# Four graph layers on one core: the order of a few TensorE steps at the layer borders

## The chip, the core and the metric

The kernel runs on 1 core of one Trainium2 chip. The metric is the time of one execution on the device in microseconds (us), as a median of several executions. The engines are named as the profile names them: PE is TensorE, DVE is VectorE, ACT is ScalarE, POOL is GpSimd, SP is SyncE (here it only issues DMAs).

## The reference

A graph of N = 3327 nodes with 512 features each and a dense 0/1 adjacency matrix goes through four layers. Each normalises the rows, applies a relu, runs a graph layer and adds the result to its input:

```python
h = relu(layernorm(x))
x = x + GAT0(h, adj)      # 8 heads of 64
h = relu(layernorm(x))
x = x + GAT1(h, adj)      # 4 heads of 128, adjacency plus the identity
h = relu(layernorm(x))
x = x + GAT2(h, adj)      # 8 heads of 64
h = relu(layernorm(x))
x = x + Mean3(h, adj)

# a head of a GAT layer
Wh = h @ W ;  s1 = Wh @ a1 ;  s2 = Wh @ a2
att = softmax over j of where(adj, leaky_relu(s1[i] + s2[j], 0.2), -inf)
out = elu(att @ Wh)

# the mean layer
agg = adj @ h / max(degree, 1)
out = relu(concat(h @ W_self + b_self, agg @ W_nb + b_nb) @ W_comb + b_comb)
```

## The kernel before

**Tiles and stages.** The nodes are 26 tiles of 128 rows (NT = 26, the last has 127), the 512 features are KC = 4 blocks of 128. A GAT layer first makes, per node tile, the projected features multiplied by exp(s2) and by exp(0.2 s2) (in three bf16 pieces, or in float32), and stores these pieces to DRAM. Then it runs over chunks of four target tiles and, inside, over the heads. For each head ACT (L694) and DVE (L691) compare s1[i] + s2[j] with zero for every source tile j, and DVE combines the outcome with the adjacency mask (`and` at L698, `xor` at L700). The two 0/1 matrices `tht` and `gt` are the stationary operands of the attention products on PE, with the pieces `ab` as moving operand: L809 and L812 in layers 0 and 2, L805 and L802 in layer 1. In layer 1 three of the five groups of source tiles are used as float32: there ACT (`ts`, L663) or DVE (`tv`) casts the 0/1 matrix first, and the products are L802. The source tiles come in groups of 6, 6, 6, 4 and 4. A chunk's four targets are worked in two passes of two; only in the first head of a layer's first chunk both passes first run over the source tiles below 22 and then over the rest, which leaves time for the last node tiles' pieces to arrive.

**The next layer's tiles.** The node work of layer l+1 is woven into the attention products of layer l. `node_stages` gives for each tile t a list of steps: load the layer's output, `statistics` (DVE, then POOL in `norm`, up to L359), `relu` (ACT, L365, makes `h`), `turn` (four PE transposes L138 into a PSUM tile `tp`, and one ACT copy L142 that makes `hT`), `projected` (eight PE matmuls in two halves of four: 264 or 272 columns with the scores, then 256 without; L420), `scaled` (ACT exponentials and DVE multiplications, L462), `parts` (the pieces on DVE, ACT and POOL), `send` (stores, issued by SP at L562). `Hooks.run` takes one step of every tile in flight between two passes. In the last chunk's run the last two tiles, 24 and 25 (NT-2 and NT-1), remain when the attention products are over: `hooks.drain()` runs their steps one after the other. This stretch between the last attention product of a layer and the first of the next one is called a border here. There are three: layer 0 to 1, 1 to 2, and 2 to 3.

**What else lies at a border.** Layer 3 is linear up to its last relu, so its weights are multiplied together ahead of time. The class `Fusion` does that, W_self @ W_comb's upper half at the first border and W_nb @ W_comb's lower half at the second. Each is four blocks of 128 rows: `block(k)` transposes a block of the weights (L138, and the copy L142), runs four matmuls of 512 columns (L191), copies the result from PSUM (L195) and stores it. `biases` is four matmuls of 512 columns (L208) whose result DVE adds to the bias (L212). Blocks 0 and 1 and the bias product stand ahead of the drain, blocks 2 and 3 behind it:

```python
        fusion = close()
        if fusion:
            for k in range(2):
                fusion.block(k, gone[-1])
            fusion.biases(gone[-1])
        adds = run_left()
        hooks.drain()
        for add in adds:
            add()
        if fusion:
            for k in range(2, KC):
                fusion.block(k, gone[-1])
```

At the third border there is no fusion. There each of tiles 22 to 25 has two projections of its own onto the multiplied weights, `project_last` with i = 1 in the tile's steps and i = 0 behind the drain (L498, four matmuls of 512 columns each). Behind them the mean layer's products start (L1077), after a small transpose (L1033).

L528 (`send_s1`) is a small transpose that turns the last chunk's scores s1 into rows. It follows tile 25's projection.

**What sets the order.** All engines' instructions are put in order at build time by a scheduler with a cost model; buffers of a pool are handed on by semaphores. `after(inst, name)` adds a dependence that only the scheduler sees: `inst` is placed behind the instruction called `name`, usually the last attention product of a pass (`gone[-1]`) or the last projection matmul (`L.mm`), and nothing waits for it at run time. On each engine the instructions then run in this fixed order, and one that waits holds up all behind it.

## Time and profile before

| | |
|---|---|
| three runs | 3471.0, 3467.43, 3469.67 us; median 3469.67 |
| the profiled execution | 3468.93 us, of which the profile's span is 3466.7 us |
| mean granted TensorE clock | 0.996 of full speed |
| busy share of the span | PE 98%, PE weight loads 89%, DVE 76%, ACT 72%, POOL 18% |
| DMA | 797.69 MB, mean 230 GB/s |
| first border (0 to 1) | from about 1167 to 1198 us of the span |
| second border (1 to 2) | from about 2012 to 2046 us |
| third border (2 to 3) | from about 3130 to 3149 us |

The times in the views are microseconds from the start of the span. A row of a timeline gives the start, the time until the group of like instructions ends, engine, line, operation, output and inputs by the program's names, sizes, the number of instructions, and in square brackets the engine's idle time just before the row with what ended it. A row of the table of windows gives the stretch, its length, the busy time of PE, PE's weight loads, DVE, ACT and POOL (with the number of rows), the granted TensorE clock as PEclk, the DMA engines' busy share and their GB/s. "Granted clock" is the share of full speed that the throttle let TensorE have.

### The profile page before, as it was taken

The numbers are of one execution on the slowest core, as the hardware profiler recorded it, in microseconds if no ns is written. First come the engines' busy times: TensorE is split into PE (matmuls) and PEld (weight loads), VectorE is DVE, ScalarE is ACT, GpSimd is POOL, SyncE is SP. The second block draws the span as 40 slices with busy tenths as digits, with TensorE's granted clock in tenths as the row PEclk, the third lists the DMA queues.
The fourth block names the chain that finished last, engine by engine and source line by source line (L and its number), as shares of the span: only waits on it lengthen the run. The fifth ranks groups of instructions, "written<-read, shape, count | busy, mean of one in ns | idle before, by whom it ended". The sixth has DMA issues, their size and how long they took to land.

```text
span 3466.7 us, 77498 instructions
## 1 busy us (share of the span) xinstructions
PE 3412.4 (98%) x30735; PEld 3092.3 (89%) x30735; DVE 2641.0 (76%) x5131; ACT 2502.6 (72%) x4125; POOL 640.6 (18%) x886
## 2 busy tenths in 40 slices
PE   8899999999999999999999999999999999999999
PEld 6799999999999788888888879989898989887887
DVE  8889888988878799889888867877776768682221
ACT  6878887878888888898888767766676757582211
POOL 7611222212111202323233320000000001021000
PEclk9999999999999999999999999999999999999999
DMA  8799999999857887787877976555555555586331
GB/s 237 237 295 279 244 268 253 259 270 261 234 194 266 294 283 259 271 287 258 287 272 268 336 258 201 190 191 162 192 175 179 185 177 186 166 299 263 104 110 55
DMA packets 398629, 797.69 MB, mean 230 GB/s; under 512 B 112969, under 2 KB 221844, under 8 KB 397616
## 3 DMA queue, kind: packets, MB, share of 16 engines
q1 hardware_dynamic: 363890, 723.14, 65.3%
q0 software_dynamic: 27488, 60.32, 7.3%
q10 hardware_dynamic: 6878, 9.18, 0.8%
q8 instruction: 244, 4.00, 0.5%
q14 instruction: 129, 1.06, 0.1%
HBM read 663.59 MB, written 129.64 MB: 229 GB/s over the span
## 4 chain that ended last, share of the span: by engine, by line
PE 90%; DVE 4%; DMA 2%; ACT 2%; issue 2%; POOL 1%; SPq 0%; ACTq 0%; POOLq 0%; DVEq 0%
PE acc L809 24%; PE acc L812 24%; PE acc L802 13%; PE acc L1077 9%; PE acc L805 6%; PE mm L420 5%; PE mm L498 5%; PE acc L420 1%; ACT gt L694 1%; PE tp L138 1%; PE mm L191 1%; DMA tr<-at 1%; DMA ab<-ab 1%; DMA w<-in_L_gnn_W_dram 0%; DVE AB L462 0%
## 5 line engine op out<-in xcount | busy, mean ns | idle before, releaser
L694 ACT ACTIVATE gt<-s1b,ks 128x512 fp8e4<-128x512 f32 (+1 forms) x2448 | 1448.2, 677 | 373.4 <-PE acc L812 262.1
L809 PE MATMUL acc<-ab,tht 128*128 128x195 bf16 (+1 forms) x9112 | 1551.2, 248 | 1.4 <-DVE deg L830 1.4
L812 PE MATMUL acc<-ab,gt 128*128 128x195 bf16 (+1 forms) x9112 | 1550.7, 248 | 1.5 <-DVE gt L700 1.5
L812 PEld LDWEIGHTS <-gt 128*128 128x128 fp8e4 x10744 | 1051.1, 98 | 22.4 <-issue 15.4
L809 PEld LDWEIGHTS <-tht 128*128 128x128 fp8e4 x10744 | 1051.2, 98 | 14.2 <-issue 5.8
L698 DVE TENSOR_TENSOR tht<-gt,m 128x768 uint32<-128x768 uint32 (+3 forms) x557 | 447.9, 804 | 101.1 <-ACT gt L694 98.6
L700 DVE TENSOR_TENSOR gt<-tht,m 128x768 uint32<-128x768 uint32 (+3 forms) x557 | 449.0, 806 | 9.5
L663 ACT CAST ts<-tht 128x1536 fp32r<-128x1536 fp8e4 x208 | 301.8, 1471 | 94.5 <-PE acc L802 87.9
L691 DVE TENSOR_SCALAR gt<-s1b,ns 128x512 fp8e4<-128x512 f32 (+1 forms) x446 | 224.9, 507 | 168.3 <-PE acc L812 167.1
L802 PE MATMUL acc<-ab,ts 128*128 128x258 f32 x2496 | 332.9, 289 | 0.6 <-DMA ab<-ab 0.4
L802 PEld LDWEIGHTS acc<-ab,ts 128*128 128x128 f32 x2496 | 312.0, 189 | 8.7 <-ACT tht L694 0.8
L925 POOL TENSOR_TENSOR xt<-xt,e 128x512 f32<-128x512 f32 x72 | 121.5, 1687 | 1053.0 <-DVE e L924 1030.0
L694 ACT ACTIVATE tht<-s1b,ks 128x512 fp8e4<-128x512 f32 (+1 forms) x504 | 309.1, 680 | 0.9 <-DMA s1b<-s 0.2
L1077 PE MATMUL acc<-y,mf 128*128 128x512 f32 x1352 | 309.6, 391 | 0.0
L1077 PEld LDWEIGHTS acc<-y,mf 128*128 128x128 f32 x1352 | 253.7, 188 | 55.7 <-issue 0.5
L812 PE MATMUL acc<-abx,gt 128*128 128x195 bf16 (+1 forms) x1632 | 283.1, 248 | 1.7 <-DVE rc L847 1.7
L809 PE MATMUL acc<-abx,tht 128*128 128x195 bf16 (+1 forms) x1632 | 283.1, 248 | 0.2 <-DVE tht L698 0.2
L827 DVE TENSOR_REDUCE R<-acc 128x130 f32<-128x390 f32 x416 | 214.4, 554 | 78.8 <-PE acc L812 77.9
L1074 ACT CAST mf<-m 128x768 fp32r<-128x768 fp8e4 (+1 forms) x78 | 59.1, 762 | 243.2 <-PE acc L1077 231.4
L805 PE MATMUL acc<-ab,tht 128*128 128x387 bf16 x1248 | 223.6, 328 | 5.9 <-DMA ab<-ab 5.9
L802 PE MATMUL acc<-ab,tv 128*128 128x258 f32 x1664 | 218.4, 283 | 0.7 <-DMA ab<-ab 0.7
L802 PEld LDWEIGHTS acc<-ab,tv 128*128 128x128 f32 x1664 | 207.1, 189 | 1.7 <-issue 0.9
(168 smaller groups left out, 3712.3 us busy)
## 6 DMA issues: line engine op xcount, KB each, us to landing
ab<-ab SPq DMA_DIRECT2D x333, 600.0 KB, 5.9
ab<-ab SPq DMA_DIRECT2D x112, 774.0 KB, 6.5
ab<-ab SPq DMA_DIRECT2D x112, 516.0 KB, 5.2
ab<-ab SPq DMA_DIRECT2D x112, 400.0 KB, 3.8
abx<-ab SPq DMA_DIRECT2D x110, 400.0 KB, 6.6
ab<-ab SPq DMA_DIRECT2D x56, 582.0 KB, 6.3
s1b<-s SPq DMA_DIRECT2D x120, 256.0 KB, 5.3
m<-mask SPq DMA_DIRECT2D x69, 384.0 KB, 4.4
```

Source lines behind the costliest of these rows:

```text
L420: mm = nc.tensor.matmul(pw, hT[:, k, :], L.w[:, k, o:e], start=(k == 0), stop=(k == KC - 1))
L663: (nc.scalar.copy if KIND[g] == "s" else nc.vector.tensor_copy)(t[:, :k1 - k0, :nj], th[a][g][:, k0:k1])
L691: nc.vector.tensor_scalar(gv[:, :, jj, :], s1v, L.ns2[:, j, h:h + 1], 2.0, op0=ALU.is_gt, op1=ALU.mult, saturate=False)
L694: nc.scalar.activation(gv[:, :, jj, :], s1v, AF.Relu, bias=L.ks2[:, j, h:h + 1], scale=BIG, saturate=False)
L698: nc.vector.tensor_tensor(pu, gu, mu, ALU.bitwise_and)
L700: nc.vector.tensor_tensor(gu, pu, mu, ALU.bitwise_xor)
L802: mm = nc.tensor.matmul(acc[k][:, :2 * DA], thr[g][:, k - ks[0], jj, :], ab[a][g][:, jj, :], start=(j == 0), stop=(j == NT - 1), skip_grou ...
L805: mm = nc.tensor.matmul(acc[k][:, :3 * DA], th[a][g][:, k, jj, :], ab[a][g][:, jj, :3 * DA], start=(j == 0), stop=(j == NT - 1), skip_grou ...
L809: nc.tensor.matmul(acc[k][:, :3 * DA + o], th[0][g][:, k, jj, :], ab[0][g][:, jj, :3 * DA + o], start=(j == 0), stop=False, skip_group_che ...
L812: mm = nc.tensor.matmul(acc[k][:, AO:AO + 3 * DA + o], th[1][g][:, k, jj, :], ab[0][g][:, jj, AO:AO + 3 * DA + o], start=False, stop=(j == ...
L827: nc.vector.tensor_reduce(R[:, k], v.rearrange("p a (s d) -> p a d s", s=3), AX.X, ALU.add)
L1077: nc.tensor.matmul(acc[k], mf[:, jj, :], y2[g][:, jj, s, :], start=(j0 + jj == 0 and s == 0), stop=(j0 + jj == NT - 1 and s == 1))
```

## The change

The change only moves PE work (with the copies and the stores that follow it); no product is added or removed.

- `transposed` notes the name of its last transpose in `turned`. `block` no longer runs its product at once: it returns a function that does, through the new method `product`, and an optional `late` places that product behind a named instruction.
- The bias product is kept in `owed` and issued by `turn` of tile NT-2, placed behind that tile's transposes.
- For tile NT-2 `projected` issues only the half with the scores. The other half is issued by `second_half` one step later, placed behind tile NT-1's transposes, and these are placed behind the first half (`L.mid`) in place of the whole projection (`L.mm`).
- Before layer 3 tile NT-2's projection with i = 1 is cut in halves of two matmuls each (`half_last`), with the same placing.
- Blocks 2 and 3 are no longer issued at the border. `blocks` hands them to the next layer's first head: both blocks' transposes are issued behind its first pass (targets 0 and 1, source tiles below 22) and both products behind its second pass (targets 2 and 3, the same source tiles).
- That head's first product is placed behind the last projection, and the PSUM tiles of a projection's two halves are taken in the opposite order.

```diff
@@ transposed
+        turned.append(tr.ins.name)
...
         def block(self, k, behind):
-            w = self.w.pop(k)
+            w = self.w[k]
             wT = transposed(w, pre, "hT", 2, behind)
+            return lambda late=None: self.product(k, w, wT, behind, late)
+
+        def product(self, k, w, wT, behind, late):
             pw = ps.tile([P, D], F32, name="mm")
             for m in range(KC):
-                nc.tensor.matmul(pw, wT[:, m, :], self.wc[:, m, :], start=(m == 0), stop=(m == KC - 1))
+                mm = nc.tensor.matmul(pw, wT[:, m, :], self.wc[:, m, :], start=(m == 0), stop=(m == KC - 1))
+                if late and m == 0:
+                    after(mm, late)
...
@@ projected
-                   for f in range(2)]
+                   for f in (1, 0)][::-1]
...
-            products(L, pws[0], hT, 0, DH2)
+            L.mid = L.mm
+            if first or t != NT - 2:
+                products(L, pws[0], hT, 0, DH2)
...
+    def half_last(L, t, hT, pw, k0):
+
+        for k in range(k0, k0 + KC // 2):
+            mm = nc.tensor.matmul(pw, hT[:, k, :], L.w[1][:, k, :], start=(k == 0), stop=(k == KC - 1))
+            if k == KC // 2:
+                after(mm, turned[-1])
+        L.mid = mm.ins.name
...
@@ node_stages
         def turn():
-            b = L.mm if t == NT - 1 and not first else behind()
+            b = L.mid if t == NT - 1 and not first else behind()
             q["hT"] = transposed(q["h"], mp, "A", A_BUFS[2], b) if late else transposed(q["h"], pool, "hT", 2, b)
+            if owed and t == NT - 2:
+                owed.pop()(turned[-1])
...
+        def first_half():
+            q["pw"] = ps.tile([P, D], F32, name="mm")
+            half_last(L, t, q["hT"], q["pw"], 0)
+
+        def second_half():
+            if L.l == 3:
+                half_last(L, t, q["hT"], q["pw"], KC // 2)
+                project_last(L, t, q["hT"], 1, pw=q["pw"])
+            else:
+                products(L, q["pw"][0], q["hT"], 0, D // 2, turned[-1])
...
         stages = [lambda: q.update(x=get_x()), statistics, relu, turn]
+        if L.l == 3 and t == NT - 2:
+            return stages + [first_half, lambda: (second_half(), own())]
...
-                         lambda: q.update(AB=scaled(L, t, q["pw"], pool, first, behind())),
+                         lambda: (t == NT - 2 and second_half(),
+                                  q.update(AB=scaled(L, t, q["pw"], pool, first, behind()))),
...
@@ attention, in the loop over passes
+                                if c == 0 and h == 0 and a == 0 and j == 0 and l:
+                                    after(first if l == 2 else mm, L.mm)
...
+                        if blocks and c == 0 and h == 0 and js[-1] < NT - 1:
+                            if ks[0] == 0:
+                                turns = [blocks[0].block(k, mm.ins.name) for k in range(2, KC)]
+                            else:
+                                blocks.pop()
+                                for product in turns:
+                                    product(mm.ins.name)
...
@@ attention, behind the last chunk
             for k in range(2):
-                fusion.block(k, gone[-1])
-            fusion.biases(gone[-1])
+                fusion.block(k, gone[-1])()
+            owed.append(fusion.biases)
...
         if fusion:
-            for k in range(2, KC):
-                fusion.block(k, gone[-1])
+            blocks.append(fusion)
```

More of the change, by code (lines that the diff above doesn't have):

```diff
@@ L161, in tile_gnn @@
     copied = []
+    turned = []
+    owed = []
     WW = D // 2 + 8
@@ L489, in parts, with project_last @@
             nc.vector.tensor_scalar(L.ns2[:, js], L.s12[:, 1, js, :], -1.0, None, op0=ALU.mult)
-    def project_last(L, t, hT, i, behind=None):
+    def half_last(L, t, hT, pw, k0):
[4 more added lines that the diff above has]
+        L.mid = mm.ins.name
+    def project_last(L, t, hT, i, behind=None, pw=None):
         n = pn(t)
@@ L495, in project_last @@
         g, jj = jwhere[t]
-        pw = ps.tile([P, D], F32, name="mm")
-        for k in range(KC):
-            mm = nc.tensor.matmul(pw, hT[:, k, :], L.w[i][:, k, :], start=(k == 0), stop=(k == KC - 1))
-            if k == 0 and behind:
-                after(mm, behind)
-        L.mm = mm.ins.name
+        if pw is None:
+            pw = ps.tile([P, D], F32, name="mm")
+            for k in range(KC):
+                mm = nc.tensor.matmul(pw, hT[:, k, :], L.w[i][:, k, :], start=(k == 0), stop=(k == KC - 1))
+                if k == 0 and behind:
+                    after(mm, behind)
         if i == 0:
@@ L808, in attention @@
                                     o = 1 if deg else 0
-                                    nc.tensor.matmul(acc[k][:, :3 * DA + o], th[0][g][:, k, jj, :],
+                                    first = nc.tensor.matmul(acc[k][:, :3 * DA + o], th[0][g][:, k, jj, :],
                                                      ab[0][g][:, jj, :3 * DA + o], start=(j == 0), stop=False,
@@ L935, in tile_gnn @@
     left = []
+    blocks = []
     def run_left():
```

## The prediction

> **What bounds the kernel now.** I read the page first, then the chain of waits for the places where the chain leaves the attention products, then the timeline of TensorE (PE) and of ScalarE (ACT) at the three layer borders, and last the table of windows for the granted clock.

> ```profile
> PE 3412.4 (98%) x30735; PEld 3092.3 (89%) x30735; DVE 2641.0 (76%) x5131; ACT 2502.6 (72%) x4125; POOL 640.6 (18%) x886
> PE 90%; DVE 4%; DMA 2%; ACT 2%; issue 2%; POOL 1%; SPq 0%; ACTq 0%; POOLq 0%; DVEq 0%
> ```

> PE is busy 98% of the span and carries 90% of the chain, so an edit that adds and removes no work can only win back idle PE time. At the first border (layer 0 to 1) the PE timeline shows how little that is (start, us, what, idle before it and its releaser):

> ```profile
> 1174.63 3.60 PE L208 MATMUL mm<-w,bv 128*128 128x512 f32 x8
> 1178.07 0.60 PE L138 MATMUL tp<-ident,h 128*128 128x128 f32 x4
> 1179.34 3.77 PE L420 MATMUL mm<-w,hT 128*128 128x264 f32 x16 [0.68 <-ACT hT L142]
> 1184.38 3.77 PE L420 MATMUL mm<-w,hT 128*128 128x264 f32 x16 [0.83 <-ACT hT L142]
> 1188.00 0.27 PE L528 MATMUL tp<-ident,s 128*8 128x128 f32 x1
> 1189.55 7.12 PE L191 MATMUL mm<-w,hT 128*128 128x512 f32 x16
> 1198.02 1.73 PE L802 MATMUL acc<-ab,ts 128*128 128x258 f32 x12
> ```

> Each projection waits for the copy of its transposed tile: 0.68 and 0.83 us. After L528 PE has no idle row until 1252. Beside it, ACT:

> ```profile
> 1176.16 0.81 ACT L365 ACTIVATE h<-A,mv 128x512 f32<-128x512 f32 x1 [1.94 <-POOL mv L359]
> 1195.69 1.46 ACT L663 CAST ts<-tht 128x1536 fp32r<-128x1536 fp8e4 x1
> ```

> The relu that makes tile 24's h waits for GpSimd's statistics and ends at 1176.97, whatever PE does; the first cast `ts` that layer 1's products need ends at 1197.15, while PE is filled until 1198 by L191. The second border:

> ```profile
> 2019.26 3.60 PE L208 MATMUL mm<-w,bv 128*128 128x512 f32 x8
> 2023.97 3.83 PE L420 MATMUL mm<-w,hT 128*128 128x272 f32 x16 [0.68 <-ACT hT L142]
> 2029.02 3.83 PE L420 MATMUL mm<-w,hT 128*128 128x272 f32 x16 [0.79 <-ACT hT L142]
> 2037.47 8.83 PE L191 MATMUL mm<-w,hT 128*128 128x512 f32 x16 [2.03 <-ACT hT L142]
> 2018.30 0.81 ACT L365 ACTIVATE h<-A,mv 128x512 f32<-128x512 f32 x1 [1.50 <-POOL mv L359]
> ```

> Here 3.50 us are idle, and the last L191 takes 8.83 us where the same 16 records took 7.12 before. The windows say why (length, busy times, then PEclk):

> ```profile
> 2035.00:2037.40 2.40, 0.45 (x6) 0.21 (x3) 2.40 (x6) 1.61 (x4) 0.21 (x1) 1.00 0.86 272
> 2037.40:2041.00 3.60, 3.52 (x5) 1.59 (x6) 3.46 (x3) 3.60 (x8) 3.22 (x2) 0.56 0.02 5
> ```

> After the gap the granted clock is 0.56 for 3.6 us: 1.71 us more.

> **The change, part by part.** The order of the changed kernel on PE is fixed by the build, so I take it as given: L191, transposes of tile 24, bias product, first half of its projection, transposes of tile 25, second half, projection of 25, L528, then attention without weight blocks.

> *First border, tiles.* The two waits go (-1.51): behind tile 24's transposes lies the bias product (3.44 us until the next start), behind tile 25's half a projection (about 1.8), against a copy of 0.6 and its hand-over. But the transposes now stand where the bias stood, at 1174.63, and h ends at 1176.97: a new wait of 2.35 us, which the bias product covered. Tile 25's h (relu about 1178.2 to 1179.0, behind the earlier copy) is in time. Sum +0.84; L528 stands at 1188.84. Bounds: +0.6 to +1.1 (a hand-over of DVE L462 to tile 25's buffer is within 0.2 of late).

> *First border, weight blocks.* Eight transposes and L191, about 8 us, go from ahead of layer 1's first products to the middle of its first head. PE's work is the same, but it was the cover for ACT. PE does the first 24 bf16 products (0.154 each: 12 take 1.85) from 1188.95 to 1192.65 and then wants `ts`. On ACT stand ahead of that cast, after relu 25 ends at 1179.0: 18 compares at 0.62 (8 take 5.01) 11.2, one hT copy 0.5, four exponentials 0.4, four casts of pt 2.3, the s1 copy 0.2, and 0.7 of waiting for tile 25's transposes. That is 1194.3, and the cast of 1.46 ends at 1195.8: PE waits 3.15 us (bounds 2.5 to 3.8 by how far ACT's pieces overlap). The next casts follow every 1.4 us against 1.57 for 12 products, so it is one wait. Sum of this border +4.0. The SP queue: a weight block keeps its `xt` buffer longer, so two loads of x stand later in the queue; the tables behind them are wanted only some 10 us later. At nothing; if that cover failed, up to 3.7 (the store L562's landing).

> *Second border.* h ends at 2019.11 and the transposes come at 2019.26: no new wait. Gone are 0.68, 0.79, 2.03 and the slow clock's 1.71: -5.2. New: tile 25's projection needs a buffer that DVE frees behind two mask operations (L698, L700, 0.95 each), 0.4 late; and layer 2's third group of masks, where PE arrives at 2035.4 (48 products of 0.084 after 2031.4) while ACT gives its last compare at 2034.6 and DVE's L698, L593, L700 end at 2037.2, with a few first products between: 1.1, and 0.2 at the fourth group. Sum -3.5 (-4.5 to -1.8).

> *Third border.* No bias and no blocks; only the halves.

> ```profile
> 3133.89 3.70 PE L498 MATMUL mm<-w,A 128*128 128x512 f32 x8 [0.68 <-ACT A L142]
> 3138.75 10.57 PE L498 MATMUL mm<-w,A 128*128 128x512 f32 x24 [0.62 <-ACT A L142]
> ```

> The 0.62 goes, the 0.68 stays: -0.6 (0 to -0.7).

> *The clock.* New gaps of 2.35 and 3.15 us stand at the first border. The trace has six gaps from 1.9 to 2.7 us after the start-up: three (1.90, 2.61, 2.03) were followed by a slow stretch and three (2.15, 1.91, 2.70) were not:

> ```profile
> 111.37 5.51 PE L420 MATMUL acc<-w,hT 128*128 128x272 f32 x16 [2.61 <-DVE AB L462]
> 90.79 3.83 PE L420 MATMUL acc<-w,hT 128*128 128x272 f32 x16 [2.15 <-DVE AB L462]
> ```

> 5.51 against 3.83 is 1.7. So each new gap costs 0 or 1.7, about evenly; one of two gives +1.7 (0 to +3.4).

> [...]

> **Sum.** +4.0 - 3.5 - 0.6 + 1.7 = +1.6 us. The profiled execution took 3468.93 (span 3466.7 and 2.2 around it), 0.74 under the median 3469.67. 3468.93 + 1.6 = 3470.5; as a median of executions 3471. That is within 0.2% (6.9 us), about what a measurement of this kernel can tell from no change.

> **Rivals.** *Casts in time, clock kept.* If ACT runs ahead at the first border and no gap is slowed, the sum is +0.8 - 3.5 - 0.6 = -3.3: 3466. For it: TensorE's rows alone show 5.6 us of idle time to win. Against it: ACT has no idle row of note from 1178.7 to 1197. Chance 0.20, still no change.

> *Slower: ACT held by a store's landing.* Tile 25's pt reuses tile 24's buffers, whose stores land 3.6 to 3.9 us after issue; the list of waits has ACT waiting there (0.8 us, L478). In the new order tile 24's stores go out at 1187.6 and 1188.3, so they land at 1191.4 and 1192.1, and ACT wants the buffers at 1192.2 and 1194. Slack 0.8. Other transfers of this window take up to 7.5; with such a landing ACT, and PE behind it, waits 3 us more, and both gaps are then slow (+3.4 in place of +1.7): +1.6 + 3.0 + 1.7 = +6.3, and with the upper bounds of the border's own terms over +7: 3477. It decides from a landing of about 8 us. Chance 0.17.

> *All the idle time won.* -1.51 - 3.50 - 1.71 - 0.62 = -7.3: 3462. It needs h of tile 24 two microseconds earlier, and the relu's wait for POOL L359 speaks against it: nothing of that chain is touched. Chance 0.05.

> That the change doesn't do what it says: at the third border it does a half only; elsewhere the order shows it in place.

> **How the numbers follow.** Forecast 0.58, first rival 0.20, both within 0.2%: 0.78; slower 0.17; faster 0.05. The range 3465 to 3477 takes in the forecast's bounds (the clock 0 to +3.4, the second border's -4.5 to -1.8) and the first rival, and leaves out the third and the further part of the second.

> **What would show it.** Right: PE L138 at the first border with a wait of about 2.3 us for ACT h L365; L802 with one of about 3 us for ACT ts L663; no idle time ahead of L420 at both borders over 0.5; L191 at 7.1 us at the second border, and only waits of DVE (L698, L700) near 2036; at the end one gap, not two. Wrong: L802 without a wait, a wait of ACT L478 over 2 us, a new DMA wait of PE in layer 1, or a slow clock at the second border.

## The result, and the profile after

The changed kernel takes 3474.74 us (median of 22 runs, 3469.3 to 3480.56) against 3468.18 (22 runs, 3465.3 to 3471.24): ratio 1.0018, 95% interval 1.0013 to 1.0024. It is slower by 6.6 us, 0.19%. The forecast was 3471, in a range of 3465 to 3477: the measured time lies in the range, but the forecast's sum had only 1.6 us of loss. The profiled execution took 3475.59, span 3473.4 against 3466.7.

In the new listing lines moved: L142 is L143, L191 is L197, L208 is L216, L365 is L373, L420 is L428, L462 is L472, L478 is L488, L498 is L504 and L517, L528 is L546, L663 is L697, L694 is L728, L698 and L700 are L732 and L734, L802 is L836, L805 is L839.

The page shows the same busy time and a chain with less PE in it (busy line, then the chain by engine):

```profile
PE 3413.9 (98%) x30735; PEld 3093.4 (89%) x30735; DVE 2639.9 (76%) x5131; ACT 2503.5 (72%) x4125; POOL 638.3 (18%) x886
PE 87%; DVE 4%; DMA 3%; issue 3%; ACT 2%; POOL 1%; SPq 0%; ACTq 0%; POOLq 0%; DVEq 0%
```

PE's busy time is 1.5 us longer and the span 6.7, so most of the loss is idle time. The PE timeline of the first border:

```profile
1168.41 7.13 PE L197 MATMUL mm<-w,hT 128*128 128x512 f32 x16 [0.37 <-ACT hT L143]
1178.00 0.66 PE L138 MATMUL tp<-ident,h 128*128 128x128 f32 x4 [2.45 <-ACT h L373]
1178.49 5.29 PE L216 MATMUL mm<-w,bv 128*128 128x512 f32 x8
1183.62 1.94 PE L428 MATMUL mm<-w,hT 128*128 128x264 f32 x8
1185.40 0.60 PE L138 MATMUL tp<-ident,h 128*128 128x128 f32 x4
1185.84 5.54 PE L428 MATMUL mm<-w,hT 128*128 128x256 f32 x24
1191.32 4.11 PE L839 MATMUL acc<-ab,tht 128*128 128x387 bf16 x24
1198.88 4.67 PE L836 MATMUL acc<-ab,ts 128*128 128x258 f32 x24 [3.44 <-ACT ts L697]
1209.69 7.03 PE L197 MATMUL mm<-w,hT 128*128 128x512 f32 x16
```

Both new waits are there: 2.45 us for tile 24's relu and 3.44 for the first cast, each with a slow stretch behind it: the granted clock is 0.50 from 1179.15 to 1182.54 and from 1199.63 to 1203.02, and 1.00 in the 3.4 us before and behind each (the bias product takes 5.29 where it took 3.60, and the 24 products of L836 take 4.67 where 24 like ones from 1220.31 on, at a clock of 1.00, take 3.19). The first L836 starts at 1198.88 where L802 started at 1198.02, almost the same time; but before, all four weight blocks were done by then, and now two of them, with 8 us of work, are still to come (against twelve attention products, 1.9 us, that came earlier). ACT in the same stretch:

```profile
1186.04 0.59 ACT L143 COPY hT<-tp 128x512 f32<-128x512 f32 x1 [2.33 <-PE tp L138]
1195.08 0.62 ACT L488 CAST pt<-AB 128x516 fp32r<-128x516 f32 x1 [0.74 <-DVE tht L725]
1197.36 5.59 ACT L697 CAST ts<-tht 128x1536 fp32r<-128x1536 fp8e4 x4
```

It waits 2.33 us for tile 25's transposes, which stand behind the slowed bias product, and 0.74 for DVE. The second border, on PE:

```profile
2021.29 7.13 PE L197 MATMUL mm<-w,hT 128*128 128x512 f32 x16 [0.24 <-ACT hT L143]
2037.05 3.83 PE L428 MATMUL mm<-w,hT 128*128 128x272 f32 x16 [0.76 <-DVE AB L472]
2046.70 0.43 PE L843 MATMUL acc<-ab,tht 128*128 128x195 bf16 x3 [1.55 <-DVE tht L732]
2048.52 0.33 PE L846 MATMUL acc<-ab,gt 128*128 128x195 bf16 x2 [0.89 <-DVE gt L734]
2060.50 7.06 PE L197 MATMUL mm<-w,hT 128*128 128x512 f32 x16
```

The waits for copies (0.68, 0.79, 2.03) are gone and the last two weight blocks run at a granted clock of 1.00 (7.06), but 3.20 us of waits for DVE came. The third border lost one of its two waits:

```profile
3141.39 1.98 PE L504 MATMUL mm<-w,A 128*128 128x512 f32 x4 [0.68 <-ACT A L143]
3145.37 10.46 PE L517 MATMUL mm<-w,A 128*128 128x512 f32 x24
```

**Where the 6.7 us of span arise.** Like rows of the two executions show it. L197 at the first border starts 0.75 later than L191 did (1168.41 against 1167.66), which the change did not make. The first product that waits for a transfer in layer 1 comes next, before and after:

```profile
1252.61 2.48 PE L805 MATMUL acc<-ab,tht 128*128 128x387 bf16 x14 [1.20 <-DMA ab<-ab]
```

```profile
1259.73 2.48 PE L839 MATMUL acc<-ab,tht 128*128 128x387 bf16 x14 [0.38 <-DMA ab<-ab]
```

It is 7.12 late: the first border costs 6.4, and would cost 7.2 had the wait for the transfer not shrunk by 0.82. At the second border L197 is 9.0 late (2021.29 against 2012.29): 1.9 more, lost in layer 1's last chunk. The windows from 1900 to 2012 show why, before and after:

```profile
1900.00:2012.00 112.00, 103.71 (x728) 89.61 (x726) 95.09 (x191) 78.19 (x133) 38.36 (x50) 1.00 0.93 345
```

```profile
1900.00:2012.00 112.00, 105.74 (x718) 91.91 (x716) 93.40 (x193) 81.24 (x137) 35.65 (x49) 0.95 0.89 329
```

Three slow stretches fell there in this execution, from 1953.97, 1984.69 and 2005.17 on, each 3.4 us at a clock of 0.50, behind waits of PE of 1.98, 1.89 and 2.22 us. The kernel before has like waits there (1.77, 1.91 and 2.70) and no slow stretch behind them. Of the experiments below e6, e7, e9 and e10 have one there, behind waits of 2.68, 2.04, 1.91 and 1.89 (twelve products take 3.10 for 2.14 in e6, fourteen of the projection 4.90 for 3.27 in e9); e8, with waits up to 2.02, and e11, with waits up to 2.74, have none. The edit moves no step there, so this part is put down to chance, as far as one profile of each kernel can tell. Tile 24's transposes at the third border are 7.5 late (3140.06 against 3132.55): the second border won 1.5. The end is 6.7 late: the third won 0.8.

### The profile page after: what moved, and what is told of

It is laid out like the page before. It is cut to its first block, busy times and chain, and to the rows that moved or that the text cites. A ratio compares the mean times of both kernels' runs of the same rounds, so it can differ in the third digit from the quotient of the medians.

```text
span 3473.4 us, 77480 instructions
## 1 busy us (share of the span) xinstructions
PE 3413.9 (98%) x30735; PEld 3093.4 (89%) x30735; DVE 2639.9 (76%) x5131; ACT 2503.5 (72%) x4125; POOL 638.3 (18%) x886
## 4 chain that ended last, share of the span: by engine, by line
PE 87%; DVE 4%; DMA 3%; issue 3%; ACT 2%; POOL 1%; SPq 0%; ACTq 0%; POOLq 0%; DVEq 0%
PE acc L846 24%; PE acc L843 24%; PE acc L836 14%; PE acc L1120 9%; PE acc L839 6%; PE mm L517 5%; PE mm L428 4%; DMA ab<-ab 1%; ACT gt L728 1%; PE tp L138 1%; PE acc L428 1%; DMA tr<-at 1%; PE mm L197 1%; DVE AB L472 1%; DVE r L400 1%
## 5 line engine op out<-in xcount | busy, mean ns | idle before, releaser
L728 ACT ACTIVATE gt<-s1b,ks 128x512 fp8e4<-128x512 f32 (+1 forms) x2448 | 1448.4, 677 | 377.1 <-PE acc L846 264.7
L732 DVE TENSOR_TENSOR tht<-gt,m 128x768 uint32<-128x768 uint32 (+3 forms) x557 | 447.6, 804 | 97.5 <-ACT gt L728 94.9
L734 DVE TENSOR_TENSOR gt<-tht,m 128x768 uint32<-128x768 uint32 (+3 forms) x557 | 449.6, 807 | 9.6
L697 ACT CAST ts<-tht 128x1536 fp32r<-128x1536 fp8e4 x208 | 302.0, 1472 | 97.9 <-PE acc L836 91.0
L836 PE MATMUL acc<-ab,ts 128*128 128x258 f32 x2496 | 336.0, 290 | 3.5 <-ACT ts L697 3.4
L836 PEld LDWEIGHTS acc<-ab,ts 128*128 128x128 f32 x2496 | 315.4, 191 | 11.8 <-ACT ts L697 3.8
L728 ACT ACTIVATE tht<-s1b,ks 128x512 fp8e4<-128x512 f32 (+1 forms) x504 | 309.1, 681 | 0.8
L839 PE MATMUL acc<-ab,tht 128*128 128x387 bf16 x1248 | 224.6, 329 | 4.7 <-DMA ab<-ab 4.6
L836 PE MATMUL acc<-ab,tv 128*128 128x258 f32 x1664 | 219.2, 284 | 0.0
L836 PEld LDWEIGHTS acc<-ab,tv 128*128 128x128 f32 x1664 | 207.9, 190 | 1.1 <-DMA ab<-ab 0.2
```

Of the source, the lines that this page charges most:

```text
L697: (nc.scalar.copy if KIND[g] == "s" else nc.vector.tensor_copy)(t[:, :k1 - k0, :nj], th[a][g][:, k0:k1])
L728: nc.scalar.activation(gv[:, :, jj, :], s1v, AF.Relu, bias=L.ks2[:, j, h:h + 1], scale=BIG, saturate=False)
L732: nc.vector.tensor_tensor(pu, gu, mu, ALU.bitwise_and)
L734: nc.vector.tensor_tensor(gu, pu, mu, ALU.bitwise_xor)
L836: mm = nc.tensor.matmul(acc[k][:, :2 * DA], thr[g][:, k - ks[0], jj, :], ab[a][g][:, jj, :], start=(j == 0), stop=(j == NT - 1), skip_grou ...
L839: mm = nc.tensor.matmul(acc[k][:, :3 * DA], th[a][g][:, k, jj, :], ab[a][g][:, jj, :3 * DA], start=(j == 0), stop=(j == NT - 1), skip_grou ...
```

## The experiments

All times are medians; the kernel before, run beside them, was at 3468.96 (e1 to e4), 3467.81 (e5 to e8) and 3467.9 (e9 to e11).

**e1_bias_back**, the bias product ahead of tile 24's transposes again, at the first border:

```diff
-            owed.append(fusion.biases)
+            if l == 0:
+                fusion.biases(gone[-1])
+            else:
+                owed.append(fusion.biases)
```

> The changed kernel with one part undone at the first border alone: the bias product stands ahead of tile 24's transposes again. Theory (the loss is made by two uncovered waits at the first border, each with a stretch of slow clock behind it): the wait of 2.45 us for the relu ahead of tile 24's transposes goes and 0.68 comes back for the copy of hT, and the slow stretch behind it (3.60 to 5.29 us for the bias product) goes: 1.8 to 3.5 us less than the changed kernel, so 3471 to 3473; the cast wait of 3.44 stays. Rival (tile 24's chain of statistics and relu paces the border in any order, so the wait only moves to a later row): no change, 3474 to 3475.

3474.91, ratio 1.0016 (1.0007 to 1.0025): nothing won, as the rival had it. PE, then ACT's one wait at this place:

```profile
1179.78 2.05 PE L428 MATMUL mm<-w,hT 128*128 128x264 f32 x8 [0.67 <-ACT hT L143]
1197.90 5.53 PE L836 MATMUL acc<-ab,ts 128*128 128x258 f32 x24 [6.19 <-ACT ts L697]
```

```profile
1192.27 0.62 ACT L488 CAST pt<-AB 128x516 fp32r<-128x516 f32 x1 [1.66 <-DMA ab<-pt]
```

The 2.45 went, 0.67 came, and the rest reappears as a longer wait for the cast, 6.19 in place of 3.44. ACT no longer waits 2.33 us for tile 25's transposes but 1.66 for a store to land, and PE gets its cast only 0.7 us earlier, counted from L197's start. The slow stretch behind the longer wait takes that back: the 24 products of L836 take 5.53 where they took 4.67. So undoing the wait for the relu alone wins nothing: PE is held by ACT's queue up to the first casts, and idles ahead of them in one piece or in two. How much earlier the cast would come without the store's landing this run does not show.

**e2_blocks_back**, weight blocks 2 and 3 at the first border again:

```diff
-        if fusion:
+        if fusion and l == 0:
+            for k in range(2, KC):
+                fusion.block(k, gone[-1])()
+        elif fusion:
             blocks.append(fusion)
```

> The changed kernel with another part undone at the first border alone: weight blocks 2 and 3 stand at the border again, ahead of layer 1's first casts. Theory: the wait of 3.44 us for ACT's first cast goes, and with it the slow stretch behind it (about 1.3): 3.4 to 4.7 us less than the changed kernel, 3470 to 3471.3; the wait of 2.45 ahead of tile 24's transposes stays. Rival (ACT is the bound through the whole first head, so that PE waits for a later cast instead): under 1 us less, 3474.

3469.28, ratio 1.0003 (0.9994 to 1.0012): the loss is gone, a little more than expected. No wait for a cast is left; the wait for the relu stays at 2.36, in this profile without a slow stretch behind it (the bias product takes 3.60):

```profile
1177.95 0.66 PE L138 MATMUL tp<-ident,h 128*128 128x128 f32 x4 [2.36 <-ACT h L373]
1178.44 3.60 PE L216 MATMUL mm<-w,bv 128*128 128x512 f32 x8
1199.42 3.18 PE L836 MATMUL acc<-ab,ts 128*128 128x258 f32 x24
```

**e3_both_back**, both edits together.

> Both undone at the first border: bias product ahead, blocks 2 and 3 at the border; halves, the second and the third border as in the changed kernel. Theory: the two parts add, idle time at the first border falls from 6.3 to about 0.7 us and no slow stretch is left there: 5.2 to 8.2 us less than the changed kernel, 3466.5 to 3469.5, level with the kernel before or 1 to 2 us under it. Rival (the moved steps cost through the order of the buffers and stores in layer 1, not through the two waits): half of that or less, 3471 or more.

3467.9, ratio 0.9998 (0.9989 to 1.0007): level with before. What the first border keeps:

```profile
1178.97 2.05 PE L428 MATMUL mm<-w,hT 128*128 128x264 f32 x8 [0.68 <-ACT hT L143]
1198.86 1.72 PE L836 MATMUL acc<-ab,ts 128*128 128x258 f32 x12 [0.78 <-ACT ts L697]
```

Most of what this kernel wins comes with the blocks: it is 1.4 us under e2 by the medians, and the two intervals overlap, so a gain of the bias product is not shown by the times.

**e4_first_only**, the change at the first border alone: for the other borders the bias product, the blocks, the order of the PSUM tiles and the undivided projections are as before:

```diff
-            owed.append(fusion.biases)
+            if l == 1:
+                fusion.biases(gone[-1])
+            else:
+                owed.append(fusion.biases)
...
-        if fusion:
+        if fusion and l == 1:
+            for k in range(2, KC):
+                fusion.block(k, gone[-1])()
+        elif fusion:
             blocks.append(fusion)
...
-            if first or t != NT - 2:
+            if first or t != NT - 2 or l == 2:
```

> The change at the first border alone; second and third border as before. Theory (the second border gains 0.3 us of idle time, 3.50 against 3.20, and one slow stretch of 1.7 in about half of the executions, the third border gains 0.62): 1 to 2.5 us more than the changed kernel, 3475.7 to 3477. Rival (the second border loses too, since waits for DVE's masks of 1.55 and 0.89 us took the place of those for the copy): under the changed kernel by 1 to 2, 3473.

3476.88, ratio 1.0023 (1.0012 to 1.0034). Its second border has the old waits (0.67, 0.78, 2.02) and its third both of its. The times put the gain of the two borders at 1.4 to 2.1 us (against the kernel before in each comparison, or median against median), with an interval that also allows none; that the loss lies at the first border alone is clear.

**e5_cast_early**, the changed kernel with the first two casts of layer 1 issued behind their own compares:

```diff
                     th[0].append(pv)
                     th[1].append(gv)
+                    if l == 1 and c == 0 and h == 0 and KIND[g] == "s":
+                        cast[g] = real(0, g, range(2), th)
...
-                                thr[g] = real(a, g, ks, th)
+                                thr[g] = cast.pop(g) if g in cast else real(a, g, ks, th)
```

> The changed kernel with one thing moved on ACT: in layer 1's first head the first two casts are issued right behind their own group's compares, so the first cast stands three compares and two pt casts earlier in ACT's order. After the first runs the theory is that ACT's whole queue up to the casts bounds the first border of the changed kernel (the first cast ended at 1197.2 to 1198.9 whether or not PE waited earlier). Then nothing is won: the wait of 3.44 goes from the first cast to the second, behind which the six compares and two pt casts now lie (about 5 us against 1.6 us of products): 3474 to 3476. Rival (the cast merely stands too late in the order, ACT has time enough): the 3.44 and its slow stretch go, 3470 to 3471.5.

3475.49, ratio 1.0018 (1.0009 to 1.0027): as the theory had it. ACT, then PE:

```profile
1191.09 1.46 ACT L697 CAST ts<-tht 128x1536 fp32r<-128x1536 fp8e4 x1
1194.26 3.78 ACT L728 ACTIVATE tht<-s1b,ks 128x512 fp8e4<-128x512 f32 x6
1197.94 4.21 ACT L697 CAST ts<-tht 128x1536 fp32r<-128x1536 fp8e4 x3
```

```profile
1199.45 2.95 PE L838 MATMUL acc<-ab,ts 128*128 128x258 f32 x12 [4.81 <-ACT ts L697]
```

The first cast is done by 1192.6, in time, and PE waits 4.81 for the second, behind six compares. Moving the first cast forward by itself wins nothing, since ACT's work up to the second cast stays the same.

**e9_one_block**, one block (2) back at the first border, block 3 left in the first head:

```diff
+        if fusion and l == 0:
+            fusion.block(2, gone[-1])()
         if fusion:
             blocks.append(fusion)
...
-                                turns = [blocks[0].block(k, mm.ins.name) for k in range(2, KC)]
+                                turns = [blocks[0].block(k, mm.ins.name) for k in range(2 if l == 2 else 3, KC)]
```

> The changed kernel with one of the two weight blocks (block 2) back at the first border, block 3 still in the first head. Theory (ACT's queue up to the casts sets the first border's end, PE work ahead of it is free as long as PE arrives earlier): about 4 us of work (four transposes 0.6, four products 3.5) go into a wait of 3.44, ACT gets two copies more (1.1), so PE waits 0.5 to 1 us for the first two casts together and no slow stretch follows: 4 us under the changed kernel, about 3470.5, within 1 us of both blocks back (3469.3 in e2_blocks_back). Rival (each block costs its own share): half way, 3472.

3467.36, ratio 1.0001 (0.9992 to 1.001): better than expected by the median, which is not firm (five of the eleven runs took 3470.2 to 3475.7, the profiled one among them). Four microseconds of cover are enough to take away the wait for the casts:

```profile
1192.61 3.70 PE L197 MATMUL mm<-w,hT 128*128 128x512 f32 x8
1196.15 2.47 PE L839 MATMUL acc<-ab,tht 128*128 128x387 bf16 x14
1198.57 1.72 PE L836 MATMUL acc<-ab,ts 128*128 128x258 f32 x12
```

The wait for the relu (2.09) and the slow bias product behind it (5.29) are still there. So of the work moved past ACT's casts only that part costs time, as far as these runs show, which leaves PE early and waiting there.

**e10_compares_on_dve**, the changed kernel with 4 of the 18 compares of that head on DVE; no PE step is moved by hand:

```diff
-            if j in GP_ON_DVE[l]:
+            if j in GP_ON_DVE[l] or getattr(L, "opening", False) and j in (4, 5, 10, 11):
...
+                L.opening = l == 1 and c == 0 and h == 0
```

> The changed kernel with 4 of the 18 compares of layer 1's first head (source tiles 4, 5, 10, 11 of the first chunk) on DVE in place of ACT. No PE step is put back. Theory (ACT's load between the last relu and the casts is the bound): ACT has 4 x 0.63 = 2.5 us less ahead of the casts, the wait of 3.44 falls under 1 and its slow stretch goes: 3.5 to 4.5 us under the changed kernel, 3470 to 3471. Rival (DVE's and-steps L732 come as late as ACT's compares, and DVE gets 1.7 us more): the wait stays over 2.5, 3473 or more.

3469.99, ratio 1.0006 (0.9997 to 1.0015), as the theory had it. Its PE at the casts:

```profile
1193.60 1.70 PE L837 MATMUL acc<-ab,ts 128*128 128x258 f32 x12
1196.37 1.71 PE L837 MATMUL acc<-ab,ts 128*128 128x258 f32 x12 [0.73 <-ACT ts L697]
```

With 2.5 us less on ACT the wait falls from 3.44 to 0.73. The scheduler also put the first cast ahead of the last two `pt` casts, as e5 does; e5 shows that this alone wins nothing (4.81 at the second cast there, 0.73 here). (In its profile 2.4 us are given back at 1257, where the wait for a transfer of `ab` is 2.78 in place of 0.38.)

**e6_products_between**, e3 with the second border's blocks arranged anew: transposes right behind the last projection, products ahead of the third group of the first pass:

```diff
-            blocks.append(fusion)
+            blocks.extend([fusion.block(k, N_.mm) for k in range(2, KC)])
...
+                            if blocks and j == JG[2][0]:
+                                while blocks:
+                                    blocks.pop(0)(mm.ins.name)
```

> As e3_both_back, and at the second border the transposes of blocks 2 and 3 stand right behind the last projection and their products between the second and third group of the first pass, where PE waits 1.54 and 0.88 us for DVE's masks. Theory (the blocks are cover for whatever PE would wait for there): both waits go and no new one for the copy of the transposes comes, since 48 products (4 us) lie between: 2.4 us under e3_both_back, 3465 to 3466. Rival (the copies and the masks share ACT and DVE, so that the waits come back at the fourth group): under 1 us, 3467 to 3468.

3463.22, ratio 0.9984 (0.9975 to 0.9993), 4.6 under before; against e3, each by its own comparison, 3.5 less where 2.4 was expected (ten of e3's eleven runs took longer than the longest of e6). The products stand where PE waited for the masks, and nothing waits behind them:

```profile
2033.46 0.60 PE L138 MATMUL tp<-ident,xt 128*128 128x128 f32 x4
2037.69 7.06 PE L197 MATMUL mm<-w,hT 128*128 128x512 f32 x16
2047.95 0.27 PE L631 MATMUL tp<-ident,ex 128*16 128x128 f32 x1
```

**e7_all** and **e8_without_split**, e6 with e5's casts; in e7 also the bias product at the first border split around tile 24's transposes:

```diff
-            for m in range(KC):
+            for m in range(KC)[:n] if n > 1 else range(KC - 1, KC):
...
+            if n == 3:
+                owed.append(lambda late: self.biases(late, 1, pb))
+                return
```

> As e6_products_between, with the first two casts issued earlier as in e5_cast_early, and the bias product at the first border split: three of its four matmuls ahead of tile 24's transposes (cover for the relu), one behind them (cover for the copy). Theory (with the blocks as cover, the last idle time at the first border, 0.68 for the copy and 0.78 for the cast, goes): 1.0 to 1.5 us under e6_products_between, 3464 to 3465, about 4 us under the kernel before. Rival (ACT bounds this border too, so that PE waits for the second cast what it saves earlier): as e6_products_between or above.

> As e7_all, but the bias product at the first border in one piece ahead of tile 24's transposes, so the 0.68 stays. Theory (each idle piece counts by itself): 0.7 us over e7_all. Rival (ACT's queue up to the casts is the bound): the same time as e7_all, the 0.68 being taken back at the casts.

3462.17, ratio 0.9981 (0.9972 to 0.999), and 3464.33, ratio 0.9989 (0.998 to 0.9998). The split takes the 0.68 away; the early casts make PE's wait at the casts longer here too (1.31 and 1.63 at the second cast, 0.28 in e6). The intervals of e6, e7 and e8 overlap, so their order is not settled by the times.

**e11_all_with_dve**, e6 with the split bias product and e10's four compares on DVE:

> e6_products_between (both parts back at the first border, products of the second border between two groups) with the bias product split 3 to 1 around tile 24's transposes as in e7_all, and the four compares on DVE in place of the earlier casts. Theory: no wait of PE for a copy (0.68) nor for a cast (0.28 in e6, 1.31 in e7) is left at the first border, about 1 us under e6_products_between: 3462 to 3462.5. Rival (with the blocks as cover ACT is not the bound, the waits just pass to DVE): as e6_products_between, 3463 or more.

3461.24, ratio 0.9983 (0.9974 to 0.9992): 6.7 us under the kernel before, and 13.2 under the changed kernel when each is set against the kernel before beside it. It is lower than both the theory and the rival had it, but its interval overlaps those of e6 to e8, so what the last step is worth is not settled by the times. At its first border PE never waits over 0.24 us:

```profile
1175.99 2.74 PE L216 MATMUL mm<-w,bv 128*128 128x512 f32 x6
1178.57 0.60 PE L138 MATMUL tp<-ident,h 128*128 128x128 f32 x4
1179.01 1.02 PE L216 MATMUL mm<-w,bv 128*128 128x512 f32 x2
1197.40 3.19 PE L843 MATMUL acc<-ab,ts 128*128 128x258 f32 x24
```

## Why the prediction was right or wrong

**First border, tiles: the wait was right, its price was not a price.** Forecast 2.35 us for the relu, measured 2.45; both waits for copies went. But e1 shows that this wait is not a cost of its own while the casts are late: with the bias product back ahead of it the time is the same. The sum allowed for that, since it counted the cast from a fixed time on ACT, but the step read as a loss of 0.84 that could be undone alone. The profiles say more when the border is measured from L197's start (L191 before) to the first product that waits for a transfer, without that wait: 83.75 us before, 90.94 changed, 91.58 in e1, 84.36 in e2, 83.66 in e3, 85.85 in e9. Where the blocks are back and no slow stretch follows, the wait for the relu costs 0.70 (e2 against e3), near the 0.84; in e9, where one follows, the border is 2.1 longer than before.

**First border, weight blocks: right, 3.15 forecast, 3.44 measured.** That the blocks were ACT's cover is shown by e2 and e9, that ACT's load is the bound by e10 and e5. (Before, what kept PE busy until 1198 was not L191 alone, which ended at 1196.67, but ten attention products behind it too.) The forecast had the cast end at 1195.8; it ended at 1198.9, 2.3 later after the 0.75 us of shift. PE came 2.0 later too (1195.44 against 1192.65, less the 0.75), since the bias product ran slowly and tile 25's transposes with it, for which ACT waited 2.33 where 0.7 was counted; the 0.74 for DVE was not counted at all. That the two errors cancelled, so that 3.44 came near 3.15, is luck.

**The clock: the mis-sized term.** "One of two gives +1.7": in the profile both gaps were slowed, with 3.4 us at a granted clock of 0.50 behind each. The wait at the casts, 3.44, 6.19 and 4.81 us in the changed kernel, e1 and e5, was followed by a slow stretch each time (24 products in 4.67 and 5.53 where 3.18 was seen in e2, 12 in 2.95 where 1.72 was seen in e3); the one at the relu, 2.45, 2.09 and 2.16 us in the changed kernel, e9 and e10, too (the bias product takes 5.29, 5.29 and 5.30), while behind 2.36 in e2 it takes 3.60. The two made 1.69 at the bias product and 1.48 at L836, 3.2 where 1.7 was counted; 4.0 + 3.2 = 7.2 is what the first border took more ahead of the wait for the transfer (90.94 against 83.75). What the first stretch costs by itself no run separates, since it also moves ACT through tile 25's transposes.

**Second border: the gain was over-sized.** Forecast -3.5, measured -1.5 in the profiles; the times of e4 put it at 1.4 to 2.1 together with the third. The waits for the masks were seen at the right place, but at 1.1 and 0.2 where 1.55 and 0.89 were measured, and the buffer at 0.4 where 0.76 was: 1.7 in all where 3.20 came. In the medians a second thing counts: the slow clock behind the 2.03 us gap was taken as lost in every execution, but e4's profile has the same gap (2.02) and no slow stretch: 15 records of its blocks take 6.70 us, where all 16 took 7.12 at the first border and 8.83 here in the kernel before. By the prediction's own count of such gaps, three slowed of six, half of the 1.71 was the fitting figure.

**Third border: right.** The 0.62 went and the 0.68 stayed.

Together: 6.4 - 1.5 - 0.8 = 4.1 from the three borders in the profiles where +1.6 was forecast, and 2.6 in the rest of that pair, where the edit moves no step (0.75 ahead of the borders, 1.9 in layer 1's last chunk). The medians differ by 6.6, interval 4.5 to 8.3. With the slow stretch at the second border counted half, the borders make 5.0, inside the interval; how the remaining 1.6 divides between slow stretches at other gaps and chance is not settled. The time stayed in the range because the range allowed for both gaps to be slowed (+3.4); the forecast within it did not, and its 78% for a time within 0.2% of the kernel before came true by a hair, 6.6 of 6.9 us.

**The rivals.** Of the slower rival one half came true, both gaps were slowed. The other half, the store's landing, did not decide in this profile: ACT was late for another reason, and its wait at the `pt` cast ended with DVE. It stands right behind, though: ACT waits for it 1.32 us in e4, which has the same first border (PE gets its cast 0.3 later there, counted from L197's start), 1.66 in e1, 1.52 in e3, 0.77 in e10. "All the idle time won" failed at the relu as argued; e11 gets there for the first border by leaving part of the bias product ahead of it.

## What to carry to other kernels

Before moving a step off the engine that is busiest, ask what it covers: at a border another engine's queue may fix the end, and then the busiest engine's work ahead of that end is free as long as it would wait there, and the same work behind it is paid in full. Waits ahead of such a point don't add, so undo them one at a time before believing the list. The best places for movable work are in front of the waits that a profile shows last, here the casts at the first border and the masks at the second.

## What was not expected of the hardware

Counted in windows of that length, laid so that the slow stretches begin at their edges, from 40 to 3440 us of the span, the two profiles together have seven windows in which PE was idle for 2.0 us or more, and a slow stretch began at the end of all seven; of eight with 1.7 to 2.0 us of idle time one began behind four; of twelve with 1.0 to 1.7, behind none. Like waits differed: in the kernel before, the wait of 2.70 us that ends at 1994.96 falls to 1.21 and 1.49 us into two windows and no slow stretch follows, while that of 2.03 at the second border lies in one and is followed by 3.41 us at 0.50. In e1 the clock is at 0.50 for 10.20 us, from within the wait of 6.19 on (length, busy times, clock):

```profile
1193.70:1203.90 10.20, 6.00 (x28) 6.00 (x29) 9.87 (x17) 9.31 (x11) 0.00 (x0) 0.50 0.88 304
```

This may also be why the times spread as they do: the changed kernel, with nine windows of 1.7 us or more of idle time in its profile, ranges over 11.3 us in its 22 runs, the kernel before, with six, over 5.9.
